# Works beside a sampling run at 7/6 of their pace from its 248th round and end by its 283rd; feed-forward's weights are loaded there

## Chip, cores and metric

The kernel runs on one core of a Trainium2 chip. The metric is the device time in microseconds (us), the median of several runs. Before the change it is 7438.36 us (three runs, 7436.6 to 7441.62). The execution that was profiled took 7427.54 us, and its span from first to last instruction is 7425.7 us.

## What is computed

Four convolution layers follow each other on x of 4 images x 256 channels x 64 x 64 points, float32. Each layer gets its group-normalised input and adds its output to x. Cut to what matters:

```
x = x + L0(gn(x))    # deformable convolution, squeeze-and-excite, feed-forward
x = x + L1(gn(x))    # linear attention with a depthwise 5x5 branch
x = x + L2(gn(x))    # 3x3 convolution with binarised weights
x = x + L3(gn(x))    # attention over 2x2 max-pooled keys and values

# in L0, after a 1x1 convolution y, its projection xp, and offsets and masks made of y:
samp = grid_sample(pad(xp), reference points + offsets)   # 9 points, 4 groups, 4 taps each
dout = sum over the 9 points of samp * mask, then a 1x1 projection
x2   = bn(y + dout)
s    = sigmoid(up(relu(down(mean of x2 over all points))))  # needs the whole image
m    = fc2(leaky_relu(fc1(x2 * s)))                         # feed-forward
out  = y + m
```

The group norm of a layer needs statistics over an image's whole input, so within one image the layers are in strict order. Different images are independent.

## The kernel before

All data of an image passes through DRAM between its stages; a stage is a Python generator that records some instructions and yields a cost. The stages of one image n are:

- `sample(n)`: the deformable sampling. It has 288 rounds. In a round (`gathered`) GpSimd issues four indirect gathers (L607) from a table into one of 7 buffers `g`, and TensorE weighs and sums them with small matmuls (L614) by weights `wm`, which ScalarE lays out two blocks of three rounds ahead (L599). After every second round ScalarE copies the sum (`at`, L619), TensorE transposes it (L624), ScalarE spreads it (L634); after every 18 rounds a block is projected (L647), added to y (L653, L654) and finished with a sum over its points (L658). At the end of the generator, what is still due of the last rounds is recorded.
- `feedforward(n)`: it opens its tile pools, loads the weights f1, f2, sd and su by four DMAs on SP's queue (L704 to L710), takes the mean over the image (L712, L713; this needs all sums of the sampling), computes the gate s by small matmuls (L716, L723) and ScalarE functions, scales f1 with it (L727), and then runs 8 blocks of fc1 (L752) and fc2 (L762).
- `layer1(n)`, the linear attention: matmuls for q, k and v (L837), long chains of depthwise multiply-adds on VectorE (L179), and an output step for each 1024 points (L938 denominator, L951, L955, L960 projection, L968, store L971).
- `second(n)`: `layer2(n)`, the 3x3 convolution, then `layer3(n)`, the pooled attention (L1315 to L1346).

The function `beside` interleaves them. It steps through the rounds of a sampling, and after round i of 288 it lets each further work advance until its recorded cost is its total cost times the share of its own stretch that has gone by; a work whose stretch is over is recorded to its end at once. `behind(n)` gives the two works of image n: feed-forward in the shares 0 to 0.22, linear attention in 0.22 to 1. So beside `sample(1)` stand the binarising of weights and the works of image 0; beside `sample(2)` the works of image 1 and `second(0)`; beside `sample(3)` the works of image 2 and `second(1)`. After `sample(3)` follows a stage of 900 steps without gathers, which begins with `feedforward(3)`, and later the rest.

```
for i, _ in enumerate(steps, 1):
    advance(i / number)
```

The instructions of TensorE, VectorE, ScalarE and GpSimd stand in the order in which they were recorded (`manual_schedule`), and each engine works through its own in order. SP, which issues the DMAs, is not in that list: the order of its queue is chosen when the program is built. What the works have not recorded by round 288 is recorded after that round's gathers, ahead of what the sampling's last rounds still need, and of the next sampling.

The tile pools of `feedforward` and `layer1` lie on the same side of the memory, so the weights of one feed-forward take the place of the linear attention's tiles before it.

Of the kernel before, what the change touches and what calls it, by code (L numbers as in the profile page):

```python
# [18 lines left out]
N, C, H, W = 4, 256, 64, 64  # L19
# [20 lines left out]
CONVOLVE, OFFSETS, BINARY = NB * 9 + 26, 60, 92  # L40
FEED = NB * 40 + 8
LINEAR, LAST = 956, 582
STEPS, BEGUN = 900, 0.22
CONV2, POOLED = 191, 376.5
CONV, SECOND = 150, 568
EPS_BN = 1e-5
# [26 lines left out]
class Net:  # L73
# [625 lines left out]
    def feedforward(self, n, ssum, st):  # L699
        nc, tc, a = self.nc, self.tc, self.a  # L700
        with tc.tile_pool(name=f"fa{n}", bufs=1, side="right") as sp, \
                tc.tile_pool(name=f"fb{n}", bufs=2, side="right") as bp:
            f1 = sp.tile([P, KT, 4 * C], F32, name="f1")
            nc.sync.dma_start(f1, a["fc1_wT"])  # L704
            f2 = sp.tile([P, 4 * KT, C], F32, name="f2")
            nc.sync.dma_start(f2, a["fc2_wT"])
            sd = sp.tile([P, KT, 64], F32, name="sd")
            nc.sync.dma_start(sd, a["se_down_wT"])
            su = sp.tile([64, C], F32, name="su")
            nc.sync.dma_start(su, a["se_up_wT"])  # L710
            mean = sp.tile([P, KT], F32, name="mean")
            nc.vector.tensor_reduce(mean, ssum, AX.X, ALU.add)  # L712
            nc.vector.tensor_scalar(mean, mean, 1.0 / HW, None, ALU.mult)  # L713
            ps = self.ps()
            for k in range(KT):
                nc.tensor.matmul(ps[0:64, 0:1], sd[:, k], mean[:, k:k + 1], start=k == 0, stop=k == KT - 1)  # L716
            dn = sp.tile([64, 1], F32, name="dn")
            nc.scalar.activation(dn, ps[0:64, 0:1], AF.Relu, bias=self.vec("se_down_b")[0:64])
            yield 2
            ex = sp.tile([P, KT], F32, name="ex")  # L720
            for m in range(KT):
                ps = self.ps()
                nc.tensor.matmul(ps[:, 0:1], su[:, m * P:(m + 1) * P], dn, start=True, stop=True)  # L723
                nc.scalar.activation(ex[:, m:m + 1], ps[:, 0:1], AF.Sigmoid, bias=self.vec("se_up_b", m))

            for k in range(KT):
                nc.scalar.activation(f1[:, k], f1[:, k], AF.Identity, scale=ex[:, k:k + 1])  # L727
            yield 6

            waits = []  # L730

            def leave():
                if waits:
                    waits.pop()()

            def hidden(hm, m, ps, t):
                nc.vector.scalar_tensor_tensor(hm[:, m], ps, self.vec("fc1_b", m), t, ALU.add, ALU.max)  # L737

            def total(b, m, ps, xy):
                nc.vector.tensor_tensor(xy[:, m], xy[:, m], ps, ALU.add)  # L740
                if m == KT - 1:
                    self.stats(st, xy, b)
                    nc.sync.dma_start(self.x3_d[n][:, :, b * 512:(b + 1) * 512], xy)

            for b in range(NB):
                x2 = self.block(bp, self.x2_d[n], b, "x2f")
                xy = self.block(bp, self.xy_d[n], b, "xyf")
                hm = bp.tile([P, 4 * KT, 512], F32, name="hm", bufs=1)
                for m in range(4 * KT):
                    ps = self.ps()  # L750
                    for k in range(KT):
                        nc.tensor.matmul(ps, f1[:, k, m * P:(m + 1) * P], x2[:, k], start=k == 0, stop=k == KT - 1)  # L752
                    t = bp.tile([P, 512], F32, name="lk")
                    nc.scalar.activation(t, ps, AF.Identity, bias=self.low1[:, m:m + 1], scale=SLOPE)  # L754
                    leave()
                    waits.append(partial(hidden, hm, m, ps, t))
                    yield 2.5
                leave()
                for m in range(KT):
                    ps = self.ps()  # L760
                    for k in range(4 * KT):
                        nc.tensor.matmul(ps, f2[:, k, m * P:(m + 1) * P], hm[:, k], start=k == 0, stop=k == 4 * KT - 1)  # L762
                        if k % 4 == 3:
                            leave()
                            yield 5
                    waits.append(partial(total, b, m, ps, xy))
            leave()
# [580 lines left out]
    def run(self):  # L1348
        self.setup()
        tile = lambda name, shape: self.cp.tile(shape, F32, name=name)  # L1350
        ssum = [tile(f"ssum{n}", [P, KT, NBLK]) for n in range(N)]
        st = {i: [tile(f"st{i}{n}", [P, KT, NB, 6]) for n in range(2)] for i in (1, 2, 3)}

        feed = lambda n: self.feedforward(n, ssum[n], st[1][n % 2])
        linear = lambda n: self.layer1(n, st[1][n % 2], st[2][n % 2])

        conv = lambda n, side="left": self.layer2(n, st[2][n % 2], st[3][n % 2], side)
        pooled = lambda n, wide=False: self.layer3(n, st[3][n % 2], wide)

        def second(n):  # L1360
            yield from conv(n)
            yield from pooled(n)

        def beside(steps, number, *works):


            spent, open_ = [0] * len(works), set(range(len(works)))

            def advance(share):
                for j in sorted(open_):  # L1370
                    work, total, lo, hi = works[j]
                    while j in open_ and lo <= share and spent[j] < total * (share - lo) / (hi - lo) or share >= hi:
                        cost = next(work, None)
                        if cost is None:
                            open_.discard(j)
                        if not cost:
                            break
                        spent[j] += cost

            for i, _ in enumerate(steps, 1):  # L1380
                advance(i / number)
            while any(works[j][3] <= 1 for j in open_):
                advance(1)

        rounds = NBLK * BR
        E = mybir.EngineType
        ordered = lambda: self.tc.manual_schedule(engines={E.PE, E.DVE, E.Activation, E.Pool})
        behind = lambda n: [(feed(n), FEED, 0, BEGUN), (linear(n), LINEAR, BEGUN, 1)]
        with self.tc.tile_pool(name="gather", bufs=2, side="left") as self.gp, \
                self.tc.tile_pool(name="samp", bufs=2, side="left") as self.sp:  # L1390
            with self.tc.tile_pool(name="pw", bufs=1, side="right") as wp, \
                    self.tc.tile_pool(name="pa", bufs=1, side="right") as sp, \
                    self.tc.tile_pool(name="pb", bufs=2, side="right") as bp:
                w = self.weights(wp)

                pads, used = [], []  # L1400
                convolved = (y for i in range(1, N) for y in self.convolve(i, w, sp, bp, pads, used))
                shifted = lambda first, last: (self.shifts(first, last, w["mw"], bp, pads, used), (last - first) * OFFSETS)
                beside(range(64), 64, (self.convolve(0, w, sp, bp, pads, used), CONVOLVE, 0, 1), (*shifted(0, 1), 0.3, 1))
                with ordered():
                    beside(self.sample(0, ssum[0]), rounds, (convolved, (N - 1) * CONVOLVE, 0, 0.96), (*shifted(1, N * NCH), 0, 1))
            with ordered():
                beside(self.sample(1, ssum[1]), rounds, (self.binarise(), BINARY, 0, 0.2), *behind(0))
                for n in range(2, N):
                    beside(self.sample(n, ssum[n]), rounds, *behind(n - 1), (second(n - 2), SECOND, BEGUN, 1))
        self.idle, self.alone, self.spare = cycle(["acc", "dp"]), True, True  # L1410
        rest = pooled(N - 2)
        with ordered():
            beside(range(STEPS), STEPS, (feed(N - 1), FEED, 0, 0.27), (linear(N - 1), LAST, 0.27, 1), (conv(N - 2), CONV2, 0.27, 0.53), (rest, POOLED, 0.53, 1.02))
        self.spare = False
        self.idle = cycle(["acc", "dp", "vk"])
        fours = self.layer2_fours(N - 1, st[2][1], st[3][1])
        beside(range(STEPS), STEPS, (fours, CONV, 0, 1), (rest, 60, 0, 1))

        self.banks = cycle(["mm", "mm", "mm", "vk"])
        for _ in pooled(N - 1, True):  # L1420
            pass
# [94 lines left out]
```

## Time and profile before

| what | us |
|---|---|
| median of the runs | 7438.36 |
| the profiled execution; its span | 7427.54; 7425.7 |
| gathers of sampling 0: first issue to last end | 138.5 to 1597.7 |
| gathers of sampling 1 | 1598.0 to 3051.3 |
| gathers of sampling 2 | 3051.6 to 4503.9 |
| gathers of sampling 3 | 4504.2 to 5976.5 |
| a round of four gathers, median | 5.0 |
| busy over the span: PE, DVE, ACT, POOL | 5885.9, 4870.1, 3564.6, 4928.8 |
| first feed-forward matmul after sampling 3 (L752) | 6031.5 |

The times of the gathers are read from the timeline, the busy times from the page. In a line of the profile stand the source line, the engine, the operation, and the tile written and read; in the timeline the line begins with its start and length, and ends with the engine's idle time before it and what ended that. PEld is TensorE's loading of weights, POOL is GpSimd, DVE is VectorE, ACT is ScalarE; SPq is an issue on SP's DMA queue. Line numbers are those of the kernel before; in the changed kernel they are higher by one from the added `yield` on, and by up to four at the end.

### The profile page before, as it was taken

How to read it: one execution, taken by the hardware profiler on the slowest of the kernel's cores; microseconds unless marked ns; L12 is line 12 of the kernel's file. 1: busy time of each engine (PE TensorE's matmuls, PEld its weight loads, DVE VectorE, ACT ScalarE, POOL GpSimd, SP SyncE). 2: the span in 40 equal slices, each digit the busy share in tenths (PEclk: the TensorE clock that was granted, in tenths of full speed). 3: DMA queues.
4: the chain of work that ended last, by engine and by line, in shares of the span. 5: the costliest groups of instructions: out<-in, count | busy, mean ns of one | idle time of the engine just before them, and what ended most of it. 6: DMA issues, size and time to landing. Idle time of an engine off the chain costs nothing. (4 is left out here: it accounts for less than half of the span.)

```text
span 7425.7 us, 98944 instructions
## 1 busy us (share of the span) xinstructions
PE 5885.9 (79%) x35584; PEld 3436.3 (46%) x35584; DVE 4870.1 (66%) x6099; ACT 3564.6 (48%) x10807; POOL 4928.8 (66%) x4850
## 2 busy tenths in 40 slices
PE   5676766569777777898877788988777889977889
PEld 2333333334433333345655444456554444844477
DVE  6455552644488777326989883269998833999863
ACT  2444444445554444455556554554565532655425
POOL 1777777777777777777777776777777710865410
PEclk7776776779877767898988889989889899988899
DMA  6564654666544445555554445555544431210141
GB/s 187 148 191 144 176 173 137 174 183 190 178 127 125 125 125 147 168 156 167 159 155 139 141 147 187 153 167 159 156 142 145 146 115 65 81 54 34 49 124 49
DMA packets 743149, 1037.48 MB, mean 140 GB/s; under 512 B 352000, under 2 KB 457856, under 8 KB 741248
## 3 DMA queue, kind: packets, MB, share of 16 engines
q0 software_dynamic: 221184, 604.27, 27.8%
q1 hardware_dynamic: 521472, 426.87, 19.0%
q8 instruction: 280, 4.59, 0.3%
q14 instruction: 213, 1.74, 0.1%
HBM read 857.44 MB, written 173.33 MB: 139 GB/s over the span
## 5 line engine op out<-in xcount | busy, mean ns | idle before, releaser
L607 POOL DMA_INDIRECT g<-tab,sl x4608 | 4403.3, 956 | 1571.9 <-issue 1285.6
L179 DVE SCALAR_TENSOR_TENSOR agg<-pad,vec,agg 128x1024 f32<-128x1024 f32 x2280 | 2934.3, 1287 | 64.3
L599 ACT ACTIVATE wm<-sl,con 128x48 f32<-128x48 f32 x6144 | 1496.1, 363 | 24.9 <-DMA sl<-sd 11.8
L614 PE MATMUL dp<-g,wm 128*32 128x128 f32 x9216 | 664.2, 317 | 312.2 <-DMA g<-tab,sl 308.7
L614 PE MATMUL acc<-g,wm 128*32 128x128 f32 x9216 | 664.2, 318 | 298.5 <-DMA g<-tab,sl 285.5
L614 PEld LDWEIGHTS dp<-g,wm 128*32 128x32 f32 x9216 | 324.4, 119 | 664.4 <-DMA g<-tab,sl 493.4
L614 PEld LDWEIGHTS acc<-g,wm 128*32 128x32 f32 x9216 | 325.3, 120 | 661.4 <-DMA g<-tab,sl 452.5
L1102 PE MATMUL ps<-xd,w 128*128 128x256 f32 x2304 | 547.1, 386 | 47.9 <-ACT kt L891 38.6
L1102 PEld LDWEIGHTS ps<-xd,w 128*128 128x128 f32 x2304 | 430.5, 193 | 131.7 <-ACT kt L891 40.3
L752 PE MATMUL ps<-x2f,f 128*128 128x512 f32 x1024 | 479.0, 613 | 4.7 <-ACT f L727 4.0
L762 PE MATMUL ps<-hm,f 128*128 128x512 f32 x1024 | 467.7, 604 | 0.0
L837 PE MATMUL ps<-xr,qw 128*128 128x512 f32 x768 | 442.8, 706 | 31.2 <-DMA xr<-x 20.9
L737 DVE SCALAR_TENSOR_TENSOR hm<-ps,vec,lk 128x512 f32<-128x512 f32 x256 | 191.5, 751 | 372.8 <-ACT lk L754 369.2
L619 ACT COPY at<-dp 128x256 f32<-128x256 f32 x288 | 107.3, 373 | 679.9 <-PE dp L614 668.6
L619 ACT COPY at<-acc 128x256 f32<-128x256 f32 x288 | 107.2, 372 | 594.0 <-PE acc L614 584.0
L754 ACT ACTIVATE lk<-ps,low 128x512 f32<-128x512 f32 x256 | 175.7, 688 | 363.1 <-PE ps L752 359.2
L1333 PE MATMUL ps<-gt,pT 128*128 128x129 f32 x2048 | 303.3, 307 | 34.4 <-ACT pT L1329 32.2
L1333 PEld LDWEIGHTS ps<-gt,pT 128*128 128x128 f32 x2048 | 286.7, 219 | 87.5 <-ACT pT L1329 48.7
L647 PE MATMUL po<-dT,ow 128*128 128x288 f32 x1024 | 299.3, 440 | 25.5 <-ACT dT L642 11.6
L1315 PE MATMUL s<-ph,th 128*128 128x512 f32 x512 | 280.7, 659 | 44.9 <-DVE ot L955 13.8
L201 POOL TENSOR_TENSOR ak<-ak,m 128x1024 f32<-128x1024 f32 x96 | 229.0, 2385 | 119.3 <-ACT m L197 115.7
L201 POOL TENSOR_TENSOR av<-av,m 128x1024 f32<-128x1024 f32 x96 | 227.8, 2373 | 113.2 <-ACT m L197 109.2
(286 smaller groups left out, 8337.6 us busy)
## 6 DMA issues: line engine op xcount, KB each, us to landing
g<-tab,sl POOLq DMA_INDIRECT x4608
x<-x SPq DMA_DIRECT2D x112, 512.0 KB
xr<-x SPq DMA_DIRECT2D x96, 512.0 KB
tab<-xo SPq DMA_DIRECT2D x192, 128.0 KB
x<-in_x SPq DMA_DIRECT2D x32, 512.0 KB
y<-yc SPq DMA_DIRECT2D x32, 512.0 KB
yb<-y SPq DMA_DIRECT2D x64, 256.0 KB
x<-yb SPq DMA_DIRECT2D x64, 256.0 KB
```

Source lines behind the costliest of these rows:

```text
L179: nc.vector.scalar_tensor_tensor(to, s, wt, acc, ALU.mult, ALU.add)
L201: nc.gpsimd.tensor_tensor(acc, acc, made[t - 1], ALU.add)
L599: nc.scalar.activation(wm[:, :, :, o], blocks[b][:, r:r + WR, G:], AF.Copy, scale=self.con("own")[:, o:o + 1])
L607: nc.gpsimd.indirect_dma_start(out=g[:, i, :], out_offset=None, in_=table, in_offset=bass.IndirectOffsetOnAxis(ap=sl.bitcast(I32)[:, r, i: ...
L614: nc.tensor.matmul(acc[32 * i:32 * i + 32, :], wm[:, r4, 4 * i + 2 * x:4 * i + 2 * x + 2, :], g[:, i, x * P:(x + 1) * P], start=x == 0, st ...
L647: nc.tensor.matmul(po[m][:, 0:BR * OB], self.ow[:, k, m * P:(m + 1) * P], dT[b][:, k].rearrange("p r o -> p (r o)"), start=k == 0, stop=k ...
L752: nc.tensor.matmul(ps, f1[:, k, m * P:(m + 1) * P], x2[:, k], start=k == 0, stop=k == KT - 1)
L762: nc.tensor.matmul(ps, f2[:, k, m * P:(m + 1) * P], hm[:, k], start=k == 0, stop=k == 4 * KT - 1)
L837: nc.tensor.matmul(ps, qw[:, k, m * P:(m + 1) * P], x[:, k], start=k == 0, stop=k == KT - 1)
L1102: nc.tensor.matmul(ps[:, e], w[:, k, t, 2 * half + e, m * P:(m + 1) * P], v[:, 2 * half + e, k, t:t + 8], start=i % 6 == 0, stop=i % 6 == 5)
L1315: nc.tensor.matmul(s[i], tv[:, 4 * b + j], ph[:, i * 512:(i + 1) * 512], start=True, stop=True)
L1333: nc.tensor.matmul(ps[:, 0:P + 1], pT[:, m], gt[:, m], start=m == 0, stop=m == 7)
```

## The change

`beside` gets a flag. With it, the share that the works see runs on at (1 - 0.86) / (0.98 - 0.86) = 7/6 of its pace once it is over 0.86, that is from round 248 on, and passes 1 in round 283. All works are then recorded to their end, and rounds 284 to 288 have none beside them. The flag is set for the samplings of images 1, 2 and 3.

The generators of feed-forward are made once, with a `yield` behind their four loads. The next image's stands in the list of works with the stretch 1 to 2 and a total of 1: it takes one step, the loads, when the share passes 1 (round 283), and goes on after the sampling, from the mean.

```
-STEPS, BEGUN = 900, 0.22
+STEPS, BEGUN, HASTE, END = 900, 0.22, 0.86, 0.98
 ...
             su = sp.tile([64, C], F32, name="su")
             nc.sync.dma_start(su, a["se_up_wT"])
+            yield 1
             mean = sp.tile([P, KT], F32, name="mean")
 ...
-        feed = lambda n: self.feedforward(n, ssum[n], st[1][n % 2])
+        feeds = [self.feedforward(n, ssum[n], st[1][n % 2]) for n in range(N)]
 ...
-        def beside(steps, number, *works):
+        def beside(steps, number, *works, ahead=False):
 ...
             for i, _ in enumerate(steps, 1):
-                advance(i / number)
+                share = i / number
+                if ahead and share > HASTE:
+                    share = HASTE + (share - HASTE) * (1 - HASTE) / (END - HASTE)
+                advance(share)
 ...
-        behind = lambda n: [(feed(n), FEED, 0, BEGUN), (linear(n), LINEAR, BEGUN, 1)]
+        behind = lambda n: [(feeds[n], FEED, 0, BEGUN), (linear(n), LINEAR, BEGUN, 1), (feeds[n + 1], 1, 1, 2)]
 ...
-                beside(self.sample(1, ssum[1]), rounds, (self.binarise(), BINARY, 0, 0.2), *behind(0))
+                beside(self.sample(1, ssum[1]), rounds, (self.binarise(), BINARY, 0, 0.2), *behind(0), ahead=True)
                 for n in range(2, N):
-                    beside(self.sample(n, ssum[n]), rounds, *behind(n - 1), (second(n - 2), SECOND, BEGUN, 1))
+                    beside(self.sample(n, ssum[n]), rounds, *behind(n - 1), (second(n - 2), SECOND, BEGUN, 1), ahead=True)
 ...
-            beside(range(STEPS), STEPS, (feed(N - 1), FEED, 0, 0.27), (linear(N - 1), LAST, 0.27, 1), ...
+            beside(range(STEPS), STEPS, (feeds[N - 1], FEED, 0, 0.27), (linear(N - 1), LAST, 0.27, 1), ...
```

More of the change, by code (lines that the diff above doesn't have):

```diff
@@ L1412, in run @@
         with ordered():
-            beside(range(STEPS), STEPS, (feed(N - 1), FEED, 0, 0.27), (linear(N - 1), LAST, 0.27, 1), (conv(N - 2), CONV2, 0.27, 0.53), (rest, POOLED, 0.53, 1.02))
+            beside(range(STEPS), STEPS, (feeds[N - 1], FEED, 0, 0.27), (linear(N - 1), LAST, 0.27, 1), (conv(N - 2), CONV2, 0.27, 0.53), (rest, POOLED, 0.53, 1.02))
         self.spare = False
```

## The prediction

> **What bounds the kernel now.** I read the page first: its costliest group is the gather.
>
> ```profile
> L607 POOL DMA_INDIRECT g<-tab,sl x4608 | 4403.3, 956 | 1571.9 <-issue 1285.6
> ```
>
> 4608 gathers are four samplings of 288 rounds of 4. One costs 0.95 us and 0.30 us of issue, so a round is 5.0 us and a sampling 1440 us; the timeline has the four samplings end at 1597.7, 3051.3, 4503.9 and 5976.5 us. While they run, GpSimd paces the kernel, unless TensorE falls so far behind that no gather buffer is free. There are 7 buffers: round r+7 may start only when the matmuls of round r are done, so the gathers stop as soon as the matmuls run more than 6 x 5.0 + 0.3 = 30.3 us behind. I call this distance the lag and read it from the timeline (end of a round's last gather to the end of its matmuls). In sampling 1 it falls back to 2.4 to 3 us nearly everywhere: the gathers bind. In samplings 2 and 3 it is 17 at round 247, 25 at round 281, 30 at the end: TensorE's queue binds, and the gathers only lean on their buffers.
>
> Second, windows over rounds 248 to 281 of samplings 2 and 3, and from there to the end of what is drained (columns: length; busy us of PE, PEld, DVE, ACT, POOL; clock; DMA):
>
> ```profile
> 4315.50:4494.30 178.80, 147.60 (x987) 83.20 (x990) 146.75 (x166) 94.44 (x307) 135.24 (x144) 0.89 0.50 148
> 5786.70:5965.50 178.80, 147.54 (x987) 83.20 (x990) 146.82 (x165) 94.36 (x307) 135.54 (x142) 0.89 0.48 146
> 5965.50:6013.20 47.70, 41.72 (x244) 21.00 (x234) 17.10 (x26) 15.61 (x38) 8.51 (x9) 0.93 0.29 100
> ```
>
> Both stretches take 178.8 us where gathers alone would take 34 x 5.0 = 170: TensorE and VectorE are each 0.82 busy and wait for each other. Third, the timeline of the border from sampling 2 to 3:
>
> ```profile
> 4552.40 1.08 PE L614 MATMUL acc<-g,wm 128*32 128x128 f32 x16 [4.95 <-ACT wm L599]
> ...
> 4553.78 0.94 POOL L607 DMA_INDIRECT g<-tab,sl  x1 [13.57 <-PE acc L614]
> ...
> 4561.22 0.56 PE L716 MATMUL ps<-mean,sd 128*64 128x1 f32 x4 [7.74 <-DMA su<-in_se_up_wT]
> ...
> 4564.49 0.94 POOL L607 DMA_INDIRECT g<-tab,sl  x1 [6.01 <-DMA xyf<-x]
> ```
>
> Sampling 3's first 18 rounds take 111.8 us instead of 90.0: 21.8 us of stall, in two parts. The first ends with its first matmuls, the second with L716, which waited for feed-forward's weights. Samplings 1 and 2 start without such a stall. Fourth, the end of sampling 3:
>
> ```profile
> 5975.51 0.95 POOL L607 DMA_INDIRECT g<-tab,sl  x1 [0.30 <-issue]
> ...
> 6005.57 0.65 PE L614 MATMUL dp<-g,wm 128*32 128x128 f32 x16
> ...
> 6010.98 1.98 PE L1343 MATMUL ps<-m,ww 128*128 128x512 f32 x4 [1.13 <-ACT m L1338]
> ...
> 6018.56 0.36 SPq L704 DMA_DIRECT2D f<-in_fc_wT  x1
> ...
> 6020.12 0.17 DVE L713 TENSOR_SCALAR mean<-mean 128x2 f32<-128x2 f32 x1
> ...
> 6027.79 0.56 PE L716 MATMUL ps<-mean,sd 128*64 128x1 f32 x4 [9.18 <-DMA su<-in_se_up_wT]
> ```
>
> The last gather is over at 5976.5, its matmuls come at 6005.6, the drained works end at 6013, and L716 could have started at 6020.3 (mean ready) but started at 6027.8. From 6050 us on TensorE shows no gap, so a shift there goes through to the end.
>
> **Nothing is removed.** The two programs hold the same instructions. The change moves works of rounds 248 to 288 and of the last flush into rounds 248 to 283 of samplings 1, 2, 3, and the four weight loads of the next feed-forward ahead of the tail of the sampling. In samplings 2 and 3 VectorE is then asked for the 147 us of the windows within 29 rounds (145 us), where it was 34 rounds. The last head of the linear attention (L938) stood after the matmuls of round 281; now it stands after round 276, with 7 rounds between it and the last drained matmul in both orders, and 5 rounds alone behind it.
>
> **The stretch up to L938.** TensorE's queue binds here, so earlier placing saves only what no longer stands before it: 5 rounds of gather matmuls. One round costs it 23.86/34 (L614) + 7.75/34 (L624) + a wait for the copy on ScalarE:
>
> ```profile
> PE acc L624 <- ACT at L619: 7.2, 4, 2.7
> ...
> PE dp L624 <- ACT at L619: 1.2, 1, 1.2
> ```
>
> with 0.9 more for the spread, 9.3/34. That is 1.20 us a round, 6.0 for five: 178.8 - 6.0 = 172.8 us. Here a page speaks: the Trainium skill, "Perfetto Trace Analysis", section Identifying the Most-Contended Engine, takes occupancy as a fair measure of how near VectorE is to its limit. By that rule the stretch could shrink until VectorE is full, 146.8 us; the highest share that this trace holds for 100 us is 0.91 (90.85 busy in 5600 to 5700), which gives 161.5. I take the row, 172.8, because in it VectorE waits 12.4 us for TensorE's scores and TensorE 7.0 for VectorE's products: neither is full, and moving works does not shorten their chain. 161.5 is a rival.
>
> **The border 2 to 3.** L938 comes at 4315.5 + 172.8 = 4488.3. The drain up to the matmuls of round 283 is that of before, 5965.5 to 6009.9 and 0.65: 45.0 us, so they end at 4533.3. Round 283's gathers would end unstalled at 4503.9 - 25.0 = 4478.9. The lag of 54.4 is 24.1 above the limit: the gathers stop for 24.1 us before they reach sampling 3. After that the first matmuls of sampling 3 are no limit (4553.5 against 4508.9 is 44.6, 14.3 above), nor is L716. So the stall of 21.8 is replaced by one of 24.1, earlier: +2.3 us. That L716 no longer waits (it saves 5.9: ScalarE's 32 columns end at 4555.9 and hold up its successor, which ran at 4561.9) isn't worth anything, because by rounds 70 to 76 the lags of samplings 2 and 3 are equal again (22.3 and 22.8 at round 71, 22.0 and 22.0 at 77) although they entered differently: from there the gathers' time decides.
>
> **The end of sampling 3.** The drain ends 6.0 earlier. Then come the 5 rounds: 0.65 + 2 x (0.56 copy and signals + 0.38 transposes + 1.28 two rounds) + 0.94 = 6.0. The transposes at 6012.8 stay where they are, and so does the mean, 6020.3. The loads are issued once the linear layer's last store is under way, some 6 us ahead of its 6011.4, with the store's own time about 6008; from issue to landing they took 6018.6 to 6027.8, 9.2 us, beside a 3 MB load (L1051) that now stands behind them. They land by 6017 and L716 starts at 6020.4: -7.4 us. If they were late, they would take this back, no more.
>
> **What else moves.** SP: the loads wait at the head of its queue for the linear layer's tiles. Behind them stand the last store of the sampling, an output store, the first x2f and xyf loads and the next image block, all needed only after the mean or 20 rounds on; the next sampling's tables (L590) stand ahead of them. Cost nothing; if they stood behind, sampling 3 could not begin before the loads are issued, near 4537 (6 us ahead of the linear layer's store of 4540.3, and the store), some 12 us late. POOL's queue has the gathers alone. Sampling 1: VectorE has 126.7 us of work in 171, gathers bind, and its lag may rise from 3 to some 20, below 30.3: nothing. A page speaks against the six bare rounds: the Trainium skill, "TensorE: Matmul & The Clock Gate", Part 1, says that an idle window of 3.4 us halves the clock until the next busy one. The windows show a clock of 0.66 at 3000 to 3025 and 1.00 at 3100 to 3150, so sampling 1 ends at the low clock already. By the rule sampling 2 would lose one cold window, about 1.7 us (an estimate from that page), at a border with 8 us of slack to the limit; by the row nothing. In samplings 2 and 3 TensorE has a backlog and is not idle.
>
> **Sum.** +2.3 - 7.4 = -5.1 us. The profiled execution took 7427.5 (span 7425.7, 1.8 around it), so 7422.4; the median of the runs stands 10.8 above it, and 7438.4 - 5.1 = 7433.3. What can be told from no change is about 0.2%, 14.9 us: 7423.5 to 7453.2.
>
> **Rivals.** (A) The denser stretch packs: 161.5 us instead of 172.8. Then everything behind comes 11.3 earlier: the stall at the border is 12.8 (-9.0), the end gains 7.4 + 11.3 = 18.7; together -28, 7411. For it: 31.3 us of TensorE's time in the stretch are gaps, and the waits for ScalarE's copy shrink when more works lie between. Against it: the chain is in order on both engines. (B) Slower: the waits take the place of the spared matmuls. Then the stretch stays at 178.8: the border costs 8.3, the end gains 1.4, and sampling 1 (171.1 in 145, lag 3 + 26 = 29, and a drain of 39 against 35) stalls for 3: +9.9, 7448. It decides against the change once each stretch grows by another 1.7 us (3 x 1.7 + 9.9 = 15); with 4 us, an eighth of the present gaps, 7460. For it: VectorE is asked for 147 in 145. (C) The works really end by round 283 and nothing stalls: the 21.8 and, of the 55 us from last gather to first feed-forward matmul (6031.5), all but some 16 are gone: -61, 7377. Against it: the lag is at its limit without any densening.
>
> **Chances.** Forecast 0.50 (its own range 7422 to 7446), A 0.26, B 0.18, C 0.06. Faster: A but for 0.02, C, 0.06 of the forecast: 0.36. Slower: B but for 0.01, and 0.01: 0.18. The rest, 0.46, is no change. The range 7406 to 7456 leaves out C, the ends of A and about half of B.
>
> **What would show it.** Right: sampling 2 ends near 4526 instead of 4503.9, the stall now in rounds 270 to 283; sampling 3 begins without one and ends near 6000; L716 follows L713 at once. Wrong: sampling 2 ends at 4515 or earlier (A), sampling 1 ends later than 3052 (B), or L716 still waits for a load.

## The result and the profile after

| | before | after |
|---|---|---|
| median of the runs, us (6 each) | 7438.2 | 7413.3 |
| lowest to highest, us | 7432.7 to 7441.6 | 7404.1 to 7419.2 |
| profiled execution; its span, us | 7427.5; 7425.7 | 7412.5; 7410.7 |

The ratio is 0.9968, with a 95% interval from 0.9957 to 0.9979: faster by 24.9 us, a third of a per cent. The forecast was 7433. The two profiled executions differ by 15.0 us only, because that of before is quicker than each of the six runs. Where the other 10 us lie no trace shows.

The page of the changed kernel shows the same gathers at the same pace:

```profile
L607 POOL DMA_INDIRECT g<-tab,sl x4608 | 4406.9, 956 | 1581.5 <-issue 1282.2
```

Windows of the changed kernel, from the matmuls of round 247 to the last head of the linear attention in samplings 2 and 3, and from there to the end of what is drained (columns as before: length; busy us of PE, PEld, DVE, ACT, POOL; clock; DMA):

```profile
4320.40:4480.70 160.30, 140.24 (x894) 76.74 (x897) 141.87 (x159) 85.30 (x268) 116.53 (x124) 0.88 0.49 143
5791.80:5949.00 157.20, 135.64 (x898) 76.35 (x897) 142.00 (x159) 85.44 (x268) 116.57 (x124) 0.92 0.49 144
5949.00:6000.80 51.80, 43.70 (x256) 20.70 (x252) 21.10 (x32) 23.60 (x70) 25.48 (x27) 0.97 0.38 117
```

The stretch that took 178.8 us takes 160 and 157. VectorE is busy for 142.0 of 157.2 us, 0.90, where it was 0.82. Six VectorE instructions (159 against 165) now stand behind the head, and the drain takes 51.8 us instead of 47.7. Up to the end of the drain the VectorE instructions are as many in both (190), so this longer stretch is the fairer comparison. Its windows, of before in sampling 3 and of the changed kernel in samplings 3 and 2:

```profile
5786.70:6013.00 226.30, 189.09 (x1224) 104.20 (x1224) 163.72 (x190) 109.98 (x343) 144.05 (x151) 0.89 0.44 136
```

```profile
5791.80:6000.80 209.00, 179.34 (x1146) 97.05 (x1146) 163.10 (x190) 109.03 (x336) 142.05 (x150) 0.93 0.46 138
4320.30:4533.60 213.30, 185.71 (x1146) 98.03 (x1146) 163.10 (x190) 109.00 (x336) 149.97 (x158) 0.90 0.49 143
```

In sampling 3 the 17.3 us have three parts. TensorE stands idle for 7.5 us less (29.7 instead of 37.2). The L614 and L624 of the five rounds that now stand behind are 6.2. And the other 525 matmuls, the same in both, ran 3.6 us quicker, at a granted clock of 0.93 instead of 0.89. In sampling 2 the clock stayed at 0.90, and the stretch is 4.3 us longer for it: e1 (below), with the same order up to here, has 208.9 us in sampling 2 at 0.93.

The border from sampling 2 to 3 in the timeline of the changed kernel:

```profile
4511.12 0.94 POOL L607 DMA_INDIRECT g<-tab,sl  x1 [5.47 <-PE dp L614]
...
4527.77 1.26 POOL L607 DMA_INDIRECT g<-tab,sl  x1 [1.95 <-PE dp L614]
...
4533.28 0.66 SPq L710 DMA_DIRECT2D su<-in_se_up_wT  x1
...
4534.48 0.95 POOL L607 DMA_INDIRECT g<-tab,sl  x1 [1.71 <-PE dp L614]
...
4550.80 0.59 PE L717 MATMUL ps<-mean,sd 128*64 128x1 f32 x4
```

Every gather that stalls here is released by matmuls of the gathers (L614), that is by its buffer. The 13.6 us wait behind the first matmuls and the wait behind L716 are gone. What is left is a stall ahead of the border: rounds 248 to 288 take 219.0 us, 14.0 more than 41 x 5.0, and the first 18 rounds of sampling 3 take 94.6 instead of 111.8.

The end of sampling 3 in the same timeline:

```profile
5988.73 0.95 POOL L607 DMA_INDIRECT g<-tab,sl  x1 [0.30 <-issue]
...
5998.78 1.98 PE L1344 MATMUL ps<-m,ww 128*128 128x512 f32 x4 [2.47 <-ACT m L1339]
...
6001.54 0.72 SPq L710 DMA_DIRECT2D su<-in_se_up_wT  x1
...
6007.60 5.84 PE L647 MATMUL po<-dT,ow 128*128 128x288 f32 x16 [1.28 <-ACT dT L642]
...
6014.94 0.17 DVE L714 TENSOR_SCALAR mean<-mean 128x2 f32<-128x2 f32 x1
6015.21 0.36 PE L717 MATMUL ps<-mean,sd 128*64 128x1 f32 x4 [1.77 <-issue]
```

The last gather ends 13.2 us later than before, and yet L717 (before: L716) starts 12.6 us earlier, 25.5 us behind the last gather where it was 51.3. It waits for no load. From there to the end the changed kernel takes 1395.5 us and before 1397.9.

The gain thus lies mostly between round 247 of sampling 3 and the gate of feed-forward. From the matmuls of round 247 (5786.7 before, 5791.8 after) to that gate it was 241.1 us and is 223.4, 17.7 less; 5.1 us were lost ahead of it and 2.4 gained behind.

### The profile page after: what moved, and what is told of

The parts are those of the page before. It is cut to its first block, busy times and chain, and to the rows that moved or that the text cites. A ratio compares the mean times of both kernels' runs of the same rounds, so it can differ in the third digit from the quotient of the medians.

```text
span 7410.7 us, 98955 instructions
## 1 busy us (share of the span) xinstructions
PE 5885.7 (79%) x35584; PEld 3424.9 (46%) x35584; DVE 4867.5 (66%) x6099; ACT 3566.2 (48%) x10807; POOL 4932.9 (67%) x4850
## 5 line engine op out<-in xcount | busy, mean ns | idle before, releaser
L614 PE MATMUL dp<-g,wm 128*32 128x128 f32 x9216 | 672.0, 317 | 309.9 <-DMA g<-tab,sl 307.1
L614 PE MATMUL acc<-g,wm 128*32 128x128 f32 x9216 | 661.5, 317 | 317.9 <-DMA g<-tab,sl 305.4
L614 PEld LDWEIGHTS dp<-g,wm 128*32 128x32 f32 x9216 | 325.7, 120 | 676.6 <-DMA g<-tab,sl 492.5
L614 PEld LDWEIGHTS acc<-g,wm 128*32 128x32 f32 x9216 | 323.8, 120 | 668.9 <-DMA g<-tab,sl 471.7
L1316 PE MATMUL s<-ph,th 128*128 128x512 f32 x512 | 285.7, 668 | 44.0 <-DVE r L1346 12.6
```

The costliest lines, as they stand in the source:

```text
L614: nc.tensor.matmul(acc[32 * i:32 * i + 32, :], wm[:, r4, 4 * i + 2 * x:4 * i + 2 * x + 2, :], g[:, i, x * P:(x + 1) * P], start=x == 0, st ...
L1316: nc.tensor.matmul(s[i], tv[:, 4 * b + j], ph[:, i * 512:(i + 1) * 512], start=True, stop=True)
```

## The experiments

Where the time went is followed by these marks, all read from the timeline of one profiled execution each, sampling 3, in us (that of e6 was 8 us quicker than its median, that of e7 6 us slower). "Stretch" runs from the matmuls of round 247 to the last head of the linear attention; "to the gate" runs from the matmuls of round 230, ahead of which the works stand alike in all rows but e3, e4 and e5, to L716.

| | median, us | ratio | stretch | to the gate | rounds 145 to 162 | first 18 rounds |
|---|---|---|---|---|---|---|
| before | 7438 | | 178.7 | 325.4 | 93.1 | 111.8 |
| changed | 7413.3 | 0.9968 | 157.2 | 307.7 | 97.3 | 94.6 |
| e1 pace alone | 7407.4 | 0.9960 | 157.2 | 311.4 | 95.9 | 92.8 |
| e2 loads alone | 7434.8 | 0.9999 | 178.7 | 324.5 | 95.7 | 110.9 |
| e3 transposes later | 7411.6 | 0.9964 | 177.6 | 320.6 | 93.5 | 106.6 |
| e4 one pace | 7435.3 | 0.9997 | | | 104.3 | 93.5 |
| e5 pace and transposes | 7392.1 | 0.9939 | 160.5 | 308.8 | 94.2 | 95.6 |
| e6 5/4 from 260 | 7426.1 | 0.9985 | 170.8 | 317.9 | 96.1 | 93.2 |
| e7 10/9 from 231 | 7437.2 | 0.9998 | | 323.9 | 98.9 | 94.9 |
| e8 changed, again | 7410.3 | 0.9963 | 157.2 | 307.6 | 96.9 | 95.2 |

The stretch of e4 and of e7 holds less work, since some of theirs stands ahead of round 247; it is left out. The 3.7 us between e1 and the changed kernel lie ahead of round 247, where the two have the same order; from there to the gate both take 223.4.

**e1: the pace without the loads.** The flag and the 7/6 stay; the `yield` behind the loads and the next feed-forward's place in the list are taken out.

```
-            yield 1
...
-        behind = lambda n: [(feeds[n], FEED, 0, BEGUN), (linear(n), LINEAR, BEGUN, 1), (feeds[n + 1], 1, 1, 2)]
+        behind = lambda n: [(feeds[n], FEED, 0, BEGUN), (linear(n), LINEAR, BEGUN, 1)]
```

> The changed kernel without the early loads: works at 7/6 of their pace from round 248, but feed-forward loads its weights together with its mean, as before. Theory P (the denser stretch packs: the change's profile has 157 to 160 us from round 247's matmuls to L938 where I had worked out 173): the pace is most of the gain, L716 waits some 8 us for its loads at the end of sampling 3, so 7413 + 8 = 7421. Theory L (the early loads bring it): within 4 us of before, 7434 to 7438. In the profile, P: the gap ahead of the transposes L624 in that stretch stays near 0.

Measured: 7407.42 us, ratio 0.9960 [0.9947, 0.9974]. The pace alone carries the whole gain. And L716 doesn't wait in e1 either (timeline of e1):

```profile
5997.28 1.14 SPq L710 DMA_DIRECT2D su<-in_se_up_wT  x1
...
6001.72 5.84 PE L647 MATMUL po<-dT,ow 128*128 128x288 f32 x16 [1.28 <-ACT dT L642]
...
6009.06 0.17 DVE L713 TENSOR_SCALAR mean<-mean 128x2 f32<-128x2 f32 x1
6009.33 0.36 PE L716 MATMUL ps<-mean,sd 128*64 128x1 f32 x4 [1.78 <-issue]
```

The loads were issued 12 us ahead of the mean although they are recorded behind the sampling. SP's queue isn't in recorded order: the sampling's last store (L661), recorded ahead of them, is issued at 6008.8.

**e2: the loads without the pace.** The loads are recorded at round 288, ahead of the drain; the pace stays 1.

```
-                if ahead and share > HASTE:
+                if False:
...
-        ... (feeds[n + 1], 1, 1, 2)]
+        ... (feeds[n + 1], 1, 0.9999, 2)]
```

> The changed kernel at the old pace: the works run as before up to round 288 and are then recorded to their end, and the next feed-forward's loads follow them, ahead of the sampling's tail. Theory P: only the wait of L716 goes, 7.4 us at the end of sampling 3 and up to 6 at the border of samplings 2 and 3: 7425 to 7431. Theory L: 7413 to 7418. The stretch from round 247 to L938 stays at 178.7 us in both.

Measured: 7434.84 us, ratio 0.9999 [0.9991, 1.0008]: nothing. The timeline of e2 says why:

```profile
6024.06 0.62 SPq L710 DMA_DIRECT2D su<-in_se_up_wT  x1
6024.29 0.17 DVE L714 TENSOR_SCALAR mean<-mean 128x2 f32<-128x2 f32 x1
6031.09 0.55 PE L717 MATMUL ps<-mean,sd 128*64 128x1 f32 x4 [8.31 <-DMA x<-yb]
```

Recorded early, the loads are still issued only when the mean is nearly ready (6022.7 to 6024.1), and L717 starts 6.8 us behind it. (The label names the store that SP issues next behind them; L717 doesn't read that.) In e1 and in e2 the first load waited for the linear layer's last store (L971 in e1, `x<-xq`), as SP's waits around the end of sampling 3 show, of e1 and of e2:

```profile
SPq L704 <- DMA x<-xq: 2.5, 1, 2.5
```

```profile
SPq L704 <- DMA x<-xq: 4.3, 1, 4.3
```

That store was issued at 5991.2 in e1 and at 6015.6 in e2. So what brings the loads forward is the early end of the linear layer, which the pace alone does.

**e3: the wait for the copy, cut down in the kernel before.** Of the two kernels' waits in the stretch, one stands out. Waits of before and of after in it (columns: who waits for whom; us in total, times, longest):

```profile
PE acc L624 <- ACT at L619: 7.2, 4, 2.7
PE pt L1327 <- ACT pe L1321: 5.2, 4, 1.8
```

```profile
PE acc L624 <- ACT at L619: 0.2, 1, 0.2
```

TensorE no longer waits for ScalarE's copy, which sits between its gather matmuls and its transposes of every second round. If that is the cause, then the same wait made smaller by other means should pack the old kernel's stretch as well. In e3 the transposes are recorded behind the matmuls of the next round instead of ahead of them, so that these stand between as well.

```
-                todo = [(2 * i + 2, partial(turned, bank, i)),
+                todo = [(2 * i + 3, partial(turned, bank, i)),
```

> The kernel before with one thing moved: the transposes L624 of a pair of rounds are recorded after the matmuls of the next round instead of ahead of them, so that more stands between ScalarE's copy and the transposes that wait for it. Pace and loads are those of before. If the packed stretch of the change comes of this wait (9.3 us ahead of L624 in 34 rounds before, 0.2 after): the wait goes here too, the stretch takes about 170 instead of 178.7 in samplings 2 and 3, and the time falls by 9 to 18 us, 7420 to 7429. If TensorE's waits only move on to the next instruction: stretch within 2 us of 178.7, time within 4 us of 7438.

Measured: 7411.60 us, ratio 0.9964 [0.9950, 0.9977], as large a gain as the change's, but not in the stretch: 177.6 us instead of 178.7. Over the whole program TensorE's waits for the copy fell from 211.5 us to 42.4, as the waits of before and of e3 show:

```profile
PE acc L624 <- ACT at L619: 124.0, 80, 9.7
...
PE dp L624 <- ACT at L619: 87.5, 71, 10.0
```

```profile
PE dp L624 <- ACT at L619: 21.6, 19, 1.7
PE acc L624 <- ACT at L619: 20.8, 16, 1.7
```

The matmuls come into round 247 of sampling 3 some 12 us earlier (5774.8 instead of 5786.7) and keep that: 2.5 us of it stand on entering sampling 3, some 5 come from its first 18 rounds and 5 from a smaller lag. In the stretch itself the wait was nearly halved and not removed, 4.7 us where it was 8.4, as the waits of e3 there show:

```profile
PE acc L624 <- ACT at L619: 4.0, 3, 1.7
...
PE dp L624 <- ACT at L619: 0.7, 1, 0.7
```

TensorE's gaps grew at other places (33.0 us in sum, 31.3 before). So that wait does cost this kernel time, and cutting it that far doesn't pack the stretch; what its full absence would do alone e3 doesn't show.

**e4: one pace throughout.** HASTE is 0: the works run at 1/0.98 from round 1, so that the last five rounds are as bare as in the change, and the loads come early as well.

```
-STEPS, BEGUN, HASTE, END = 900, 0.22, 0.86, 0.98
+STEPS, BEGUN, HASTE, END = 900, 0.22, 0.0, 0.98
```

> The changed kernel with HASTE 0: the works run at 1/0.98 of their pace from the first round on and still end by round 283, six bare rounds and early loads included. If the six bare rounds and the loads are what counts: 7413, as the change. If it is the density of the stretch from round 248: the stretch has 7/6 less density than in the change, takes 170 to 178, and of the change's 25 us about the 8 to 14 of the loads stay: 7424 to 7430.

Measured: 7435.30 us, ratio 0.9997 [0.9989, 1.0005]. The bare rounds and the early loads don't carry the gain by themselves. Sampling 3 begins without the old stall (93.5), but rounds 145 to 162, already the tightest place behind the border, now take 104.3 us instead of 93.1, and 104.2 instead of 95.8 in sampling 2. Together these 19.6 us are more than the 18.3 gained at the border. Since this pace costs time earlier in each sampling, e4 doesn't tell what the bare rounds are worth alone.

**e5: pace and later transposes together.** e1 with the edit of e3.

> The dense pace alone (as in e1, 7407.4) together with the later turning of e3 (7411.6). If the two gains have different sources (the dense stretch for the pace, the lag carried through the whole sampling for the turning), they add for the most part: 30.6 + 26.4 less what both take from the border and the end, some 7380 to 7395, with rounds 248 to the last head at 157 to 160 us and a lag at round 247 near 12. If both gains are the same thing (the gathers stop at their buffers less), the second adds little: 7400 to 7412.

Measured: 7392.05 us (7391.05 to 7392.95), ratio 0.9939 [0.9926, 0.9953]: 44 us below before, faster than either kernel here, and faster than e1 or e3 (0.9960 and 0.9964; the slowest run of e5, 7393.0, lies below the quickest of e1, 7403.8). The two gains add for the greater part: 44 of 31 + 26. The windows line of the stretch of e5:

```profile
5767.90:5928.50 160.60, 139.92 (x902) 76.62 (x902) 143.07 (x159) 86.47 (x269) 120.52 (x128) 0.89 0.49 145
```

The stretch is packed as in the change, and it begins 19 us earlier than before (5767.9).

**e6 and e7: other paces to the same end.** If a denser order packs in general, then so should 5/4 from round 260 and 10/9 from round 231, both at the end by round 283. (The expectations name the round before, since 0.90 and 0.80 of 288 are 259.2 and 230.4.)

```
-STEPS, BEGUN, HASTE, END = 900, 0.22, 0.86, 0.98
+STEPS, BEGUN, HASTE, END = 900, 0.22, 0.90, 0.98
```

This is e6 against e1; e7 has 0.80.

> The pace alone, but from round 259 at 5/4 (to 98% of the rounds). Theory V (VectorE's share in the dense stretch goes to 0.88 to 0.92 whenever the works lie densely enough): share at least 0.88 in the dense stretch, time 7405 to 7420. Theory O (the packing of the change is the luck of one order of instructions): share anywhere from 0.82 to 0.90, time 7405 to 7440.

> The pace alone, but from round 230 at 10/9 (to 98% of the rounds). Theory V: share of VectorE at least 0.88 in the dense stretch, time 7405 to 7420. Theory O: share anywhere from 0.82 to 0.90, time 7405 to 7440. By the forecast's row (a round spared gives back 1.2 us of TensorE's queue and no more) each sampling saves 6 us as in the forecast, about 7432.

Measured: 7426.14 us in e6, ratio 0.9985 [0.9978, 0.9991], and 7437.21 us in e7, ratio 0.9998 [0.9990, 1.0006]. Less than half of the change's gain, and none. Windows from the matmuls of round 230 to the last head, of before, of the change and of e7:

```profile
5702.40:5965.40 263.00, 216.91 (x1475) 122.15 (x1478) 218.09 (x251) 146.19 (x471) 199.40 (x209) 0.90 0.50 149
```

```profile
5707.50:5949.00 241.50, 205.12 (x1386) 115.35 (x1385) 213.32 (x245) 137.37 (x433) 180.45 (x191) 0.93 0.51 149
```

```profile
5721.50:5977.20 255.70, 209.54 (x1387) 116.63 (x1387) 217.26 (x251) 138.16 (x437) 181.63 (x191) 0.93 0.48 143
```

VectorE's share is 0.83, 0.88 and 0.85. In e7 the denser works only ran up a lag: the gathers stand 30.8 us ahead of the matmuls at round 247 (18.6 in the change), at the limit, for the rest of the sampling. The waits of e7 in the same window, and those of e6 from round 247 on, show what has come in place of the copy:

```profile
PE pt L1327 <- ACT pe L1321: 11.5, 4, 7.3
...
PE acc L624 <- ACT at L619: 3.1, 3, 1.6
```

```profile
PE pt L1327 <- ACT pe L1321: 10.3, 4, 7.0
...
PE acc L624 <- ACT at L619: 2.7, 1, 2.7
```

The wait for the copy shrank in both, to 5.2 and 3.9 us with the matmuls into `dp`, from 9.4 and 8.4. But TensorE's wait for the pooled attention's exponentials (L1321), 5.2 us before in either window, has grown to 11.5 and 10.3. In the change that wait is nearly gone together with the other: of TensorE's gaps in the stretch 0.2 us lie before L624 and 0.9 before L1328, where before it was 9.3 and 6.0.

e6 is mixed on the theory that VectorE fills up. Its dense part alone, rounds 259 on, is fuller than anything in the change, 0.94, and still gains little, because the old order was full there already (0.88), as the windows of before and of e6 for those rounds show:

```profile
5854.40:5965.40 111.00, 89.19 (x630) 52.31 (x632) 98.07 (x108) 60.15 (x198) 84.14 (x88) 0.86 0.51 155
```

```profile
5853.60:5956.70 103.10, 82.50 (x561) 47.43 (x564) 97.03 (x108) 53.02 (x167) 69.79 (x74) 0.92 0.48 145
```

Nor is TensorE's idle time up to the end of the drain smaller: 36.8 us in e6 where it was 37.2. What e6 saves there, 7.1 of 226.3 us, is little more than the matmuls of the five rounds:

```profile
5785.90:6005.10 219.20, 182.39 (x1142) 99.20 (x1146) 163.23 (x190) 108.20 (x336) 143.49 (x151) 0.92 0.44 132
```

The room was in rounds 248 to 258, where the old order has VectorE busy for 48.7 of 67.7 us, 0.72. The change fills those too (62.0 of 69.3, 0.89). So what is gained depends on where the pace sets in. That it depends on which instruction comes to stand next to which is read from the waits.

**e8: the changed kernel again.**

> The changed kernel once more, beside the other paces. If the early loads cost what lies between e1 (7407.4) and the changed kernel (7413.3), it comes out again some 6 us above the pace alone, 7411 to 7416; if that was the scatter of the runs, anywhere from 7404 to 7416.

Measured: 7410.34 us, ratio 0.9963 [0.9949, 0.9976]. Between 7413.3 and 7407.4, with overlapping intervals: a cost of the early loads can't be told from none.

**e9 to e12: begun three rounds earlier or later, the pace again, six buffers.** e9 and e10 are e1 with HASTE and END at 0.85 and 0.9786, and at 0.87 and 0.9814: 7/6 again, from another round. e11 is e1. e12 is the changed kernel with `bufs=6` for `g`.

> The pace alone, 7/6 as in the changed kernel, but begun three rounds earlier (share 0.85, full at 0.9786 of the rounds). Theory F (7/6 is a pace at which works and rounds fit into each other): waits of the accumulating matmuls for ScalarE's copy under 1 us in the dense stretch, from the matmuls of round 230 to the mean's matmul of image 3 in 307 to 312 us, time 7405 to 7415. Theory O (luck of one order): another wait for ScalarE or VectorE takes the place of the one gone, 315 to 325 us as in the paces 10/9 and 5/4, time 7416 to 7440.

> As e9, begun three rounds later instead (share 0.87, full at 0.9814). Theory F: as in e9, 307 to 312 us and 7405 to 7415. Theory O: 315 to 325 us in one at least of e9 and this, time 7416 to 7440 there.

> e1 once more. Theory F and theory O both expect 7404 to 7412 (e1: 7407.4). If the early loads cost time, it stays 3 to 6 us below the changed kernel (7413.3 and 7410.3); if not, the two overlap.

> The changed kernel with 6 buffers for the gathers instead of 7: they stop at a lag of 25.3 us instead of 30.3. If the stall at the limit is what sets a sampling's end, each place that reaches the limit gives 5 us more: rounds 145 to 162 and the border of sampling 2, and rounds 145 to 162 of sampling 3, some +15, 7424 to 7430. If the matmuls' queue alone sets the end and the gathers only follow it, nothing: 7406 to 7416.

These four can't be read by their expected times: the chip that they ran on took 8579.0 us for the kernel before, 15% more. Their ratios to it are 0.9949 [0.9936, 0.9961], 0.9971 [0.9960, 0.9982], 0.9957 [0.9944, 0.9970] and 0.9946 [0.9934, 0.9958]. The pace is thus worth as much there as in e1 (0.9960). The gathers themselves are as quick as elsewhere, but stand still far more (page of e11):

```profile
L607 POOL DMA_INDIRECT g<-tab,sl x4608 | 4398.0, 954 | 2723.3 <-issue 1195.8
```

A round takes some 6.0 us instead of 5.0 in all four samplings, with a median lag of 30.2 us even in sampling 0, where the profiled execution of before has 3.0. There the gathers stand at the limit of their buffers from sampling 0 on, so the border is no place of its own and the question of six buffers, asked for a kernel that reaches its limit in two places, wasn't answered: with one buffer less the change was no slower than e11 there, and no run there has the changed kernel with seven.

One reading holds within that chip. TensorE's waits for the copy ahead of L624 in the stretches of samplings 2 and 3 are none in e11 and 0.2 us at most in e12, which have the change's order, but 1.4 and 2.1 in e9 and 5.9 and 4.4 in e10. (All gaps before L624 are 6.7 and 7.3 in e9, 5.9 and 8.6 in e10.) Theory F asked for less than 1. So there the pace 7/6 alone doesn't spare this wait; the change's order does, and three rounds to either side bring some of it back. But the time doesn't follow the wait: e9 is not slower than e11, and e10 by 7 us, within the intervals. And the gaps before L1327, 0.9 us in the change, are 7.4 and 8.2 in e11, though the order is the same.

## Why the prediction was right or wrong

**The sum and the range.** The time lay in the range and on the faster side, to which the forecast had given 0.36, and in the place of rival A (7411), to which it gave 0.26; no change had the largest share, 0.46. The range held because it had been drawn down to rival A, and not by the forecast's own working: that was luck. The forecast's own number, 7433, was 20 us too high. Half of that is the profile that it was built on: the offset of 10.8 us between the profiled execution of before and the median was added to the result, while the profiled execution of after stands 0.8 below its median. The other half, 7422.4 against 7412.5, is in the steps. Of the signs, sampling 2 ended at 4520.8, between the forecast's 4526 and rival A's 4515.

**The stretch up to L938: the step that failed.** The forecast took 1.20 us of TensorE's queue for each of five rounds, 172.8 us; measured 160.3 and 157.2. It weighed this row against the rule of the Trainium skill, "Perfetto Trace Analysis", section Identifying the Most-Contended Engine, which with a share of 0.91 gave 161.5, and took the row, since moving works doesn't shorten their chain. In this kernel it did: the waits of the old order, for the copy and for the exponentials, had nearly gone in the new one. The five rounds themselves were sized well (6.0 us, measured 6.2). What the forecast left as it was is the waits, 7.5 us less, and the clock, 3.6 us: it put the end of the drain 220.3 us behind round 247, and it came at 209.0. The rule was right for this order (0.885, 0.90, and 0.89 in e5). But the row is what e6 measured: 170.8 us, and from round 230 to the gate 317.9 us, as much as before needs up to its mean (6020.3 - 5702.4), where the forecast had left it. And in e7 VectorE had the room and didn't fill up. Neither argument could tell beforehand which of the two orders this would be. The instruction order of the new program was there to be read; the forecast counted what stood before L938 and not which instruction stood next to which.

**The border.** A stall of 24.1 us ahead of the border was to replace 21.8; measured were 14.0 in rounds 248 to 288 and 4.6 at the start of sampling 3, against 0.8 and 21.8. The formula comes near with the measured stretch in it: 18.5 us of lag at round 247, 160.4 to the head and 46.8 to the matmuls of round 283 (forecast 45.0), less 36 x 5.0 for the gathers, leave 45.7, which is 15.4 above the limit of 30.3. The place was off: of the 14.0 us, 5.8 lie in rounds 270 to 283 and 6.7 in the bare rounds behind them. But of the 4.0 us gained there nothing arrived: sampling 3 loses 4.2 more in its rounds 145 to 162, and its matmuls reach round 247 2.4 us later than before in e8 and 5.1 us later in the first profile, 2.5 of which it had on entering sampling 2. The forecast had said +2.3, by a sum that didn't hold, so this is luck. That a stall at the border is worth little because the lag evens out later was right: at round 144 of sampling 3 it is 30.1 us in both profiles; rival A's -9.0 for it was not.

**The end.** "The transposes at 6012.8 stay where they are, and so does the mean" was wrong, and is the same step again: the drain ended 11 us before its forecast, and transposes, projection and mean all moved with it. From round 247 to the gate it is 223.4 us; the forecast had 233.7. From the end of the drain to the gate it is 14.5 us and was 14.8: what the loads no longer hold up is taken by the five rounds alone and a slower projection. L717 followed the mean at once, as forecast, but not for the reason given: e1 has that without the early loads, and e2 doesn't have it with them. "From 6050 us on TensorE shows no gap" was misread (it is idle for 174 us there in before, with the first gap over 1 us at 6256.7), but the shift did go through to the end.

**Free steps.** Sampling 1 ended at 3053.8 and, in e8, at 3050.1 (3051.3 before), with a lag of 3.0 at round 247: nothing, as forecast. The first of these is past the 3052 that was to show rival B, but without B's stall: B fell. SP's other queue entries cost nothing that e8 beside e1 could show. Rival C's freedom from stall didn't come: 18.6 us of stall stay.

**The clock.** "In samplings 2 and 3 TensorE has a backlog and is not idle" was wrong for the end of both. In sampling 3 the last projection took 5.84 us (as in e1) where it had been 4.15, on the path: 1.7 us of the gain given back. Windows of the two kernels over these 16 matmuls, before and after (the column behind POOL's is the granted clock):

```profile
6014.50:6018.70 4.20, 4.11 (x16) 2.92 (x16) 0.54 (x3) 0.69 (x2) 0.00 (x0) 1.00 0.94 321
```

```profile
6007.60:6013.50 5.90, 5.83 (x16) 4.01 (x16) 0.52 (x3) 0.69 (x2) 0.00 (x0) 0.71 0.76 288
```

In sampling 2 the four matmuls of L1344 took 3.68 us, while they take 1.98 in sampling 3 and in sampling 2 of e1, and the gather at 4534.48 stalled for 1.71 us until the L614 behind them was done (timeline of the changed kernel):

```profile
4529.93 3.68 PE L1344 MATMUL ps<-m,ww 128*128 128x512 f32 x4 [2.47 <-ACT m L1339]
```

Both are the size that the forecast had estimated for sampling 2 from the Trainium skill, "TensorE: Matmul & The Clock Gate", Part 1. It preferred its row, by which nothing would be lost, on a reading that sampling 1 ends at the low clock; yet the window from 3025 to 3051 shows 0.87. (The bare rounds that it calls six there are the five of its sum.)

**What stays open.** Why this order, and not its neighbours, lets both waits vanish is not shown; it was not derived from the two programs' orders. How much of the gain the copy's wait is worth stays open too: on the slower chip e9 gains as much with part of it back. And why one sampling ran at a clock of 0.90 and another of the same order at 0.93 is not known. That TensorE's waits for the exponentials (10.3 us in e6, 11.5 in e7) are what keeps those two orders from packing is argued from the waits; no run moved L1321. The gain of e3 was followed to its place (ahead of round 248), and what makes its first 18 rounds shorter is open.

## What to carry to other kernels

Where engines that work in order feed each other, a denser order can be worth much or nothing: the same works ended by the same round gave 25 us, 10 us and nothing here. So read the new order for each pair of producer and consumer, and try other paces before a reason is given. Occupancy says how far a stretch can shrink and not that it will; look first where in the stretch the share is low (0.72 in eleven rounds here), and push work there. And put the matmuls of one more round between a copy and the transposes that read it: that alone was worth as much here as the whole change, and both together more than either.

## What the runs showed of the hardware

- TensorE's clock fell with no idle gap over 2.5 us. In sampling 3 of the changed kernel no gap between TensorE's matmuls from 5998.8 to 6007.6 exceeds 1.3 us, and the one before is 2.5; it was 0.64 busy at the full clock in the window from 6003 to 6006, and the clock was 0.82 and 0.61 in the next two. In sampling 2 it fell ahead of the bare rounds, behind a window with 0.53 us of matmuls in 3: L1344 took 3.68 us instead of 1.98, and the last projection, 10 us later, 4.15. Windows of 3 us of the changed kernel, first of sampling 3, then of sampling 2:

```profile
6003.00:6006.00 3.00, 1.91 (x48) 1.20 (x40) 0.00 (x0) 1.26 (x4) 0.00 (x0) 1.00 1.04 412
6006.00:6009.00 3.00, 1.72 (x6) 1.14 (x7) 0.39 (x1) 0.72 (x3) 0.00 (x0) 0.82 0.93 285
6009.00:6012.00 3.00, 3.00 (x9) 2.18 (x8) 0.47 (x2) 0.00 (x0) 0.00 (x0) 0.61 1.03 399
```

```profile
4527.00:4530.00 3.00, 0.53 (x17) 0.27 (x9) 1.96 (x4) 0.98 (x3) 1.93 (x2) 0.99 0.22 72
4530.00:4533.00 3.00, 3.00 (x4) 1.10 (x4) 0.69 (x1) 1.69 (x4) 2.17 (x3) 0.50 0.78 243
```

- One chip took 15% longer for the same program (the kernel before, 8579 us against 7436), with gathers of 954 ns like the others and a mean clock of 0.80 against 0.85. Its traces release GpSimd's gathers (749 us) and ScalarE's copies (1599 us) by events that they don't attribute to an engine of the core, some of them 11 us behind the recorded end of the matmuls; what held these up is not known.
